# A selective scan over eight images a step in pairs: 128x1024 elementwise instructions, 16-step blocks and one shared double bank for rank-one terms

## The chip, the core and the metric

The kernel runs on one core of a Trainium2 chip. A core has engines that work side by side, each through its own list of instructions in order: TensorE (PE, with its weight loads PEld) for matmuls, VectorE (DVE), ScalarE (ACT) and GpSimd (POOL) for elementwise work, and SyncE (SP), which here issues most DMAs. They wait for one another through semaphores. Matmuls write PSUM[...]; the other tiles lie in SBUF. The metric is the device time of one execution in microseconds (us).

## What is computed

The input is eight images of 128 channels and 64 x 64 pixels. A layer with a deformable 3 x 3 convolution comes first: group norm, an offset convolution, bilinear gathers at the shifted positions, a convolution over nine taps, and a residual. Its result is read as 4096 tokens of 128 channels per image. Then a state-space scan runs over the tokens of each image, and last a mixture of eight experts, two of which are taken for each token.

```python
xs, z = jnp.split(x_proj, 2, axis=-1)            # x_proj = norm(t) @ W_in
delta = xs @ W_delta; Bv = xs @ W_B; Cv = xs @ W_C
deltaA = jnp.exp(jnp.einsum('bld,dn->bldn', delta, A))
deltaB = jnp.einsum('bld,bln->bldn', delta, Bv)
def step(state, inp):                             # state: images x 256 (d) x 256 (n)
    state = dA_i * state + dB_i * x_i[:, None, :]
    y = jnp.einsum('bdn,bn->bd', state, C_i)
y = y * silu(z);  t = t + y @ W_out
```

What takes the time is the scan: 4096 steps for every image, each of which multiplies a state of 256 x 256 values by decays, adds a term, and contracts the result with C.

## The kernel before

**Stages.** `prepare` and `images` run first. They build the gather table, offsets and weights of the deformable convolution for all images, and take the first 1.7 ms. Then the scan runs, for four images at a time (`QI = 4`), twice, each time over 128 blocks of 32 tokens (`BL = 32`). A block of 4 x 32 = 128 tokens fills the 128 partitions of the token work: `conv` gathers and convolves two blocks ahead, `project` computes xs, z, delta, B and C for the next block, and `behind` does the gate, the output projection, the router and the experts for the block before. A hardware loop covers `BODY = 32` blocks per pass, all written out.

**State and tiles.** The state index n lies on partitions, in two halves (`NH = 2`), and d (`DIN = 256`) along a row. So the state of one image is 128 x 512 fp32, one PSUM bank in size. The states of images 0, 1 and 2 are SBUF tiles `ht`; that of image 3 stays in PSUM, in `up[3]`.

**One step.**
- `decay` (L877, L883) computes dA. A matmul of `rt` (delta in three bf16 parts) with `alhs` (A in three bf16 parts) writes one of three rotating PSUM `bank`s, and ACT's Exp writes `et`. Nineteen such groups of 14 values of d serve one chunk, which is 16 (step, image) pairs; the groups are done one chunk ahead.
- `product` (L903) is `mt = et * h`, 128x512 per image. POOL does images 0 to 2, DVE image 3.
- `unit` (L897) computes the added term, B times delta times x, as a matmul with a contracted length of 9 (three by three bf16 parts) into the image's bank `up[b]`. The factors of image b lie on partitions 32b to 32b+8 of `ul` and `ur`. One call serves two images, in turn.
- `add` (L908) is `h = mt + up`, on DVE, 128x512 per image.
- `contract` (L916) adds C times `mt` into `yp`. Its stationary operand `zc` is a window of 32 columns that is zero except for one, which holds C; that column is chosen so that the result lands on the partition of this token. The part of the output that comes from the added term is put in later, through `qt` in `behind`.

**Order.** The order on each engine is written out by hand in `scan_block`: a step is cut into `NSLOT = 6` slots, each of which takes a decay group and one turn of the token work (`Work.step`, whose generators say with `yield n` how many slots later they go on). Between them stand the adds, contractions and rank-one terms. DMAs for the next chunk's factors (`load_u`, `load_r`) are issued on SP at a chunk's first step. `take` and `free` hand the three banks to token work and decays alike.

Of the kernel before, what the change touches and what calls it, by code (L numbers as in the profile page):

```python
# [23 lines left out]
FP = mybir.dt.float32  # L25
# [6 lines left out]
P = 128  # L32
# [7 lines left out]
DIN = 256  # L40
# [3 lines left out]
QI = 4  # L44
BL = 32
CH = 4
# [6 lines left out]
KR = 9 * GD  # L53
QP = 3
# [3 lines left out]
NSLOT = 6  # L58
# [6 lines left out]
def kernel(  # L65
# [76 lines left out]

    bp = [dram.tile([QI, 3, 3, BL, DIN], BF, name=f"bp{k}") for k in range(2)]
    dp = [dram.tile([QI, 3, 3, BL, DIN], BF, name=f"dp{k}") for k in range(2)]

# [266 lines left out]
    def several(n, shape, dt, name):  # L412
        return [fix.tile(shape, dt, name=f"{name}{k}") for k in range(n)]


    et = several(2, [P, NH, CH, QI, DIN], FP, "et")
    mt = several(3, [P, NH, QI, DIN], FP, "mt")
    ht = several(QP, [P, NH, DIN], FP, "ht")
    rt = several(2, [KR, RROW], BF, "rt")

    ul = several(2, [P, CH, DIN], BF, "ul")
    ur = several(2, [P, CH, DIN], BF, "ur")
    zc = several(2, [P, BL + 2, 32], FP, "zc")
# [6 lines left out]
    up = [psf.tile([P, NH, DIN], FP, name=f"up{k}") for k in range(QI)]  # L430
# [3 lines left out]
    for k in range(2):  # L434
        nc.vector.memset(ul[k], 0.0)
        nc.vector.memset(ur[k], 0.0)
        nc.gpsimd.memset(zc[k], 0.0)
# [16 lines left out]
    class Work:  # L454
# [3 lines left out]
        def add(self, gen, at=0):  # L458
            self.threads.append([gen, at])
# [139 lines left out]
    def project(k):  # L599
# [41 lines left out]
        for b in range(QI):  # L641
            for i in range(3):
                nc.sync.dma_start(
                    out=dp[k][b, i].rearrange("j l n -> l j n"),
                    in_=dpt[BL * b : BL * b + BL],
                )
# [48 lines left out]
        for b in range(QI):  # L695
            for j in range(3):
                nc.sync.dma_start(
                    out=bp[k][b, :, j].rearrange("i l n -> l i n"),
                    in_=bpt[BL * b : BL * b + BL],
                )  # L700
# [22 lines left out]
    def behind(b0, l0, k, kt):  # L723
# [40 lines left out]
        pr = wk[:, :NEXP]  # L764
        nc.vector.tensor_add(pr, pr, rb_sb)
        mx = one.tile([P, 1], FP, name="mx")
        nc.vector.tensor_reduce(mx, pr, AX.X, ALU.max)
        nc.vector.tensor_scalar(pr, pr, mx, None, ALU.subtract)
        yield 2
        nc.scalar.activation(pr, pr, AF.Exp)  # L770
        yield LAG
        sm = one.tile([P, 1], FP, name="sm")
        nc.vector.tensor_reduce(sm, pr, AX.X, ALU.add)
        nc.vector.reciprocal(sm, sm)
        nc.vector.tensor_scalar(pr, pr, sm, None, ALU.mult)
        yield 1
        top = one.tile([P, 2], FP, name="top")
        at = one.tile([P, 2], FP, name="at")
        hit = one.tile([P, NEXP], FP, name="hit")
        for kk in range(2):  # L780

            nc.vector.tensor_reduce(top[:, kk : kk + 1], pr, AX.X, ALU.max)
            nc.vector.scalar_tensor_tensor(
                hit, pr, top[:, kk : kk + 1], rank, ALU.is_equal, ALU.mult
            )
            nc.vector.tensor_reduce(at[:, kk : kk + 1], hit, AX.X, ALU.max)
            yield 1
            if kk == 0:

                nc.vector.tensor_scalar(hit, rank, at[:, 0:1], None, ALU.is_equal)  # L790
                nc.vector.scalar_tensor_tensor(pr, hit, -2.0, pr, ALU.mult, ALU.add)
                yield 1
        nc.vector.tensor_reduce(sm, top, AX.X, ALU.add)
        nc.vector.reciprocal(sm, sm)
        nc.vector.tensor_scalar(top, top, sm, None, ALU.mult)
        yield 1
        nc.vector.tensor_scalar(
            pr, rank, at[:, 0:1], top[:, 0:1], ALU.is_equal, ALU.mult
        )
        nc.vector.tensor_scalar(  # L800
            hit, rank, at[:, 1:2], top[:, 1:2], ALU.is_equal, ALU.mult
        )
        gate = one.tile([P, NEXP], FP, name="gate")
        nc.vector.tensor_add(gate, pr, hit)  # L804
# [48 lines left out]
    def load_u(k, c):  # L853
        rows = slice(CH * c, CH * c + CH)
        for b in range(QI):
            for dst, src in ((ul, bp), (ur, dp)):
                nc.sync.dma_start(
                    out=dst[c % 2][32 * b : 32 * b + 9],
                    in_=src[k][b, :, :, rows, :].rearrange("i j l n -> (i j) l n"),
                )  # L860

    def copy_c(k, c):

        nc.scalar.copy(
            zc[c % 2].rearrange("p s x -> p (s x)")[:, 31 : 31 + 32 * BL].rearrange(
                "p (s x) -> p s x", x=32
            )[:, :, 0].rearrange("p (m l) -> p m l", l=CH),
            ctt[k].rearrange("p h (b c l) -> p (h b) c l", b=QI, l=CH)[:, :, c, :],
        )

    def decay(c, g):

        n = min(GD, DIN - GD * g)
        ps = banks.pop(0)
        rv = rt[c % 2].rearrange("p (q g t) -> p q g t", q=GD, t=CT)[:, :n, g, :]
        for h in range(NH):
            nc.tensor.matmul(  # L877
                ps[:, n * CT * h : n * CT * h + n * CT].rearrange(
                    "p (q t) -> p q t", q=n
                ),  # L880
                alhs[:KR, g, P * h : P * h + P], rv, start=True, stop=True,
            )
        nc.scalar.activation(  # L883
            et[c % 2][:, :, :, :, GD * g : GD * g + n].rearrange(
                "p h l b d -> p h (l b) d"
            ),
            ps[:, : 2 * n * CT].rearrange("p (h d t) -> p h t d", h=NH, d=n),
            AF.Exp,
        )
        banks.append(ps)  # L890

    def unit(c, lo, images):

        for h in range(NH):
            for b in images:
                rows = slice(32 * b, 32 * b + 9)
                nc.tensor.matmul(  # L897
                    up[b][:, h], ul[c % 2][rows, lo, P * h : P * h + P],
                    ur[c % 2][rows, lo, :], start=True, stop=True,
                )  # L900

    def product(eng, m, c, lo, b):
        eng.tensor_tensor(  # L903
            mt[m][:, :, b], et[c % 2][:, :, lo, b], ht[b] if b < QP else up[b], ALU.mult
        )

    def add(m, b):
        nc.vector.tensor_tensor(  # L908
            ht[b] if b < QP else up[b], mt[m][:, :, b], up[b], ALU.add
        )  # L910

    def contract(m, lo, cpar, j):
        for h in range(NH):
            for b in range(QI):
                s0 = 32 * (CH * (QI * h + b) + lo) + 31 - j
                nc.tensor.matmul(  # L916
                    yp[32 * b : 32 * b + 32, :DIN],
                    zc[cpar].rearrange("p s x -> p (s x)")[:, s0 : s0 + 32],
                    mt[m][:, h, b, :],
                    start=(j == 0 and h == 0), stop=(j == BL - 1 and h == NH - 1),  # L920
                )

    def after(k, c, n):

        return ((k + (c + n) // NCH) % 2, (c + n) % NCH)
# [3 lines left out]
    def buf(j):  # L929

        n = BODY * BL
        return 1 if j == n - 1 and j % 3 == 0 else j % n % 3

    def scan_block(s, work):

        k = s % 2
        for c in range(NCH):
            for lo in range(CH):
                j = CH * c + lo
                m, m1 = buf(BL * s + j), buf(BL * s + j + 1)  # L940
                cn, ln = (c, lo + 1) if lo + 1 < CH else (c + 1, 0)
                if lo == 0:
                    load_u(*after(k, c, 1))
                    load_r(*after(k, c, 2))
                for b in range(QP):
                    product(nc.gpsimd, m, c, lo, b)

                def slot(s):
                    g = NSLOT * lo + s
                    if g < NG:  # L950
                        decay((c + 1) % NCH, g)
                    work(NSLOT * j + s)

                add(m, 0)
                slot(0)
                add(m, 1)
                if last:
                    contract(*last.pop())
                slot(1)
                unit(c % 2, lo, (2, 3))  # L960
                slot(2)
                if lo == 0:
                    copy_c(*after(k, c, 1))
                add(m, 2)
                slot(3)
                unit(cn % 2, ln, (0, 1))
                add(m, 3)
                slot(4)
                product(nc.vector, m1, cn, ln, 3)
                slot(5)  # L970
                last.append((m, lo, c % 2, j))
# [5 lines left out]
    for b0 in range(0, NB, QI):  # L977
# [4 lines left out]
        for b in range(QP):  # L982
            nc.vector.memset(ht[b], 0.0)
        nc.vector.memset(up[3], 0.0)
# [6 lines left out]
        product(nc.vector, 0, 0, 0, 3)  # L991
        unit(0, 0, (0, 1))
# [57 lines left out]
```

## Time and profile before

| | |
|---|---|
| median of 3 runs | 40915.19 us (40786.07 to 40924.38) |
| profiled execution | 40839.57 us, its span 40837.8 us |
| busy share of the span | PE 88%, POOL 81%, DVE 73%, ACT 60% |
| mean granted TensorE clock | 0.914 |
| first and last add of the scan (L908) | 1727 us and 40803 us into the span |
| DMA | 3935 MB, mean busy share of the 16 engines about 0.33 |

In the profile a line such as `L916 PE MATMUL yp<-mt,zc ... x131072 | 9629.5, 415` names the source line, engine, operation, output and inputs, and the number of instructions; behind the bar stand the time in which at least one of them was running (us) and the mean duration of one (ns), then the engine's idle time just before them and what ended it. Matmuls are pipelined: their durations overlap, and how long one keeps PE from the next is seen from the distance of starts in the timeline.

### The profile page before, as it was taken

How to read it: one execution, taken by the hardware profiler on the slowest of the kernel's cores; microseconds unless marked ns; L12 is line 12 of the kernel's file. 1: busy time of each engine (PE TensorE's matmuls, PEld its weight loads, DVE VectorE, ACT ScalarE, POOL GpSimd, SP SyncE). 2: the span in 40 equal slices, each digit the busy share in tenths (PEclk: the TensorE clock that was granted, in tenths of full speed). 3: DMA queues.
4: the chain of work that ended last, by engine and by line, in shares of the span. 5: the costliest groups of instructions: out<-in, count | busy, mean ns of one | idle time of the engine just before them, and what ended most of it. 6: DMA issues, size and time to landing. Idle time of an engine off the chain costs nothing. (4 is left out here: it accounts for less than half of the span.)

```text
span 40837.8 us, 930352 instructions
## 1 busy us (share of the span) xinstructions
PE 35932.1 (88%) x339020; PEld 18203.8 (45%) x339020; DVE 29992.8 (73%) x57416; ACT 24575.6 (60%) x61837; POOL 33028.2 (81%) x26997
## 2 busy tenths in 40 slices
PE   3599998999988999899989999889998999989898
PEld 1244444444444444444444444444444444444444
DVE  1377777777777777777777777777777777777777
ACT  0266666666666666666666666666666666666666
POOL 0388888888888888888878888888888888888888
PEclk7799999999999999999989999999999999999999
DMA  3333333333333333333333333333333333333333
GB/s 87 82 98 96 96 98 95 99 97 97 97 97 100 96 96 98 97 96 100 97 97 97 96 97 99 95 99 98 97 97 97 96 95 97 97 94 98 100 99 92
DMA packets 3069459, 3935.38 MB, mean 96 GB/s; under 512 B 1764375, under 2 KB 2499040, under 8 KB 2804848
## 3 DMA queue, kind: packets, MB, share of 16 engines
q1 hardware_dynamic: 2797344, 3200.76, 26.9%
q0 software_dynamic: 187200, 613.57, 5.2%
q10 hardware_dynamic: 80328, 61.56, 0.6%
q8 instruction: 2675, 43.83, 0.5%
q14 instruction: 1912, 15.66, 0.1%
HBM read 3276.01 MB, written 598.31 MB: 95 GB/s over the span
## 5 line engine op out<-in xcount | busy, mean ns | idle before, releaser
L903 POOL TENSOR_TENSOR mt<-et,ht 128x512 f32<-128x512 f32 x24576 | 30657.2, 1275 | 5715.9 <-DVE ht L908 4556.4
L883 ACT ACTIVATE et<-bank 128x448 f32<-128x448 f32 (+1 forms) x38950 | 19947.9, 537 | 10341.7 <-PE bank L877 9450.6
L908 DVE TENSOR_TENSOR ht<-mt,up 128x512 f32<-128x512 f32 x24576 | 16236.0, 682 | 8427.5 <-PE up L897 7118.0
L877 PE MATMUL bank<-rt,alhs 126*128 126x224 bf16 (+1 forms) x77900 | 13427.6, 266 | 2371.5 <-ACT et L883 1147.7
L877 PEld LDWEIGHTS <-alhs 126*128 126x128 bf16 x77900 | 6094.4, 99 | 10397.5 <-issue 9937.4
L916 PE MATMUL yp<-mt,zc 128*32 128x256 f32 x131072 | 9629.5, 415 | 0.0
L897 PE MATMUL up<-ur,ul 9*128 9x256 bf16 x65544 | 6919.2, 284 | 763.1 <-DVE ht L908 429.3
L903 DVE TENSOR_TENSOR mt<-et,up 128x512 f32<-128x512 f32 x8194 | 5618.5, 686 | 430.7 <-ACT et L883 26.6
L908 DVE TENSOR_TENSOR up<-mt,up 128x512 f32<-128x512 f32 x8192 | 5638.4, 688 | 4.2 <-PE bank L877 4.2
L916 PEld LDWEIGHTS yp<-mt,zc 128*32 128x32 f32 x131072 | 3687.0, 115 | 3130.1 <-issue 1326.3
L897 PEld LDWEIGHTS <-ul 9*128 9x128 bf16 x65544 | 1973.8, 93 | 4834.8 <-issue 4459.1
L574 PE MATMUL bank<-ident,w 128*128 128x128 f32 x18720 | 3390.5, 307 | 442.4 <-ACT et L883 312.7
L566 ACT ACTIVATE w<-g,rec 128x128 f32<-128x128 f32 x9360 | 3622.5, 397 | 125.7 <-DMA g<-table,rec 120.4
L574 PEld LDWEIGHTS bank<-ident,w 128*128 128x128 f32 x18720 | 2620.1, 202 | 1210.2 <-ACT et L883 565.8
L545 POOL DMA_INDIRECT g<-table,rec x2340 | 2312.3, 988 | 463.5 <-issue 207.5
L658 PE MATMUL bank<-xst,wdelta_sb 128*32 128x128 f32 x20640 | 1821.2, 426 | 67.1 <-ACT et L883 67.1
L580 ACT COPY vt<-bank 128x128 f32<-128x128 f32 x2340 | 618.8, 264 | 1914.2 <-PE bank L574 1868.2
L818 ACT ACTIVATE se<-bank,gate 128x128 f32<-128x128 f32 x2048 | 714.9, 364 | 446.3 <-PE bank L812 372.6
L289 POOL MEMSET xpad<- 128x66 f32 x8 | 1.2, 153 | 1210.8 <-POOLq L256 1210.8
L812 PE MATMUL bank<-ew_sb,tn2t 128*128 128x256 f32 x2048 | 918.7, 544 | 32.3 <-DVE gate L804 21.7
L277 PE MATMUL gm_ps<-mv,gavg 128*128 128x1 f32 x16 | 4.5, 347 | 906.9 <-DVE mv L275 906.9
L522 PE MATMUL bank<-wconv_sb,vt 128*128 128x128 f32 x4680 | 708.4, 287 | 0.0
(200 smaller groups left out, 16661.2 us busy)
## 6 DMA issues: line engine op xcount, KB each, us to landing
rt<-rz SPq DMA_DIRECT2D x2052, 1102.5 KB
rz<-dst SPq DMA_DIRECT2D x3096, 52.5 KB
dp<-dpt SPq DMA_DIRECT2D x3096, 48.0 KB
bp<-bpt SPq DMA_DIRECT2D x3096, 48.0 KB
ul<-bp SPq DMA_DIRECT2D x8200, 18.0 KB
ur<-dp SPq DMA_DIRECT2D x8200, 18.0 KB
g<-table,rec POOLq DMA_INDIRECT x2340
table<-xtok SPq DMA_DIRECT2D x256, 128.0 KB
```

Of the source, the lines that this page charges most:

```text
L545: nc.gpsimd.indirect_dma_start(out=g, out_offset=None, in_=table, in_offset=bass.IndirectOffsetOnAxis(ap=rec.bitcast(I32)[:, j : j + 1], a ...
L566: nc.scalar.activation(w[:, P * q : P * q + P], g[:, P * q : P * q + P], AF.Copy, scale=rec[:, c0 : c0 + 1],)
L574: nc.tensor.matmul(wk[:, :P], w[:, P * q : P * q + P], ident, start=(q == 0), stop=(q == 3),)
L658: nc.tensor.matmul(wk[32 * a : 32 * a + 32, P * gg : P * gg + P], wdelta_sb[:, h, d0 : d0 + 32], xlb[:, h], start=(h == 0), stop=(h == 1),)
L812: nc.tensor.matmul(wk[:, :DIN], tn2t, ew_sb[:, DIN * hf : DIN * hf + DIN], start=True, stop=True,)
L818: nc.scalar.activation(se[:, ex, :], wk[:, P * j : P * j + P], AF.Copy, scale=gate[:, ex : ex + 1],)
L877: nc.tensor.matmul(ps[:, n * CT * h : n * CT * h + n * CT].rearrange("p (q t) -> p q t", q=n), alhs[:KR, g, P * h : P * h + P], rv, start= ...
L883: nc.scalar.activation(et[c % 2][:, :, :, :, GD * g : GD * g + n].rearrange("p h l b d -> p h (l b) d"), ps[:, : 2 * n * CT].rearrange("p ...
L897: nc.tensor.matmul(up[b][:, h], ul[c % 2][rows, lo, P * h : P * h + P], ur[c % 2][rows, lo, :], start=True, stop=True,)
L903: eng.tensor_tensor(mt[m][:, :, b], et[c % 2][:, :, lo, b], ht[b] if b < QP else up[b], ALU.mult)
L908: nc.vector.tensor_tensor(ht[b] if b < QP else up[b], mt[m][:, :, b], up[b], ALU.add)
L916: nc.tensor.matmul(yp[32 * b : 32 * b + 32, :DIN], zc[cpar].rearrange("p s x -> p (s x)")[:, s0 : s0 + 32], mt[m][:, h, b, :], start=(j == ...
```

## The change

All eight images now go through the scan at once, in four pairs, and blocks are 16 steps long, so that a block is still 128 tokens. There are 4096 steps of eight images in place of 8192 steps of four. `product` and `add` handle two images in one 128x1024 instruction. POOL does pairs 0 to 2; pair 3 keeps its state in two PSUM banks `ud`. The rank-one terms of pairs 0, 1 and 2 all go through the same two banks, `up`, one pair after another, where each image had a bank before. The factors of both images of a pair lie on the same nine partitions, 32p to 32p+8, of one tile `uu`. `contract` is called for each pair, and writes rows 32p to 32p+31 of `yp`: 16 rows for each image. `mt` becomes four tiles of a pair each, and `md` for pair 3. A chunk is two steps of eight images, so a decay group still covers 16 (step, image) pairs; a step has 12 slots. In the router, small tiles move into PSUM, and two masks are kept instead of two ranks. The start of the scan, with a block of token work on its own, runs once instead of twice.

```diff
-QI = 4
-BL = 32
-CH = 4
+QI = 8
+BL = 16
+CH = 2
...
-NSLOT = 6
+NSLOT = 12
...
-    et = several(2, [P, NH, CH, QI, DIN], FP, "et")
-    mt = several(3, [P, NH, QI, DIN], FP, "mt")
-    ht = several(QP, [P, NH, DIN], FP, "ht")
+    et = several(2, [P, CH, QI, NH, DIN], FP, "et")
+    mt = several(4, [P, 2, NH, DIN], FP, "mt")
+    md = fix.tile([P, 2, NH, DIN], FP, name="md")
+    ht = several(QP, [P, 2, NH, DIN], FP, "ht")
...
-    up = [psf.tile([P, NH, DIN], FP, name=f"up{k}") for k in range(QI)]
+    ud = psf.tile([P, 2, NH, DIN], FP, name="ud")
+    up = psf.tile([P, 2, NH, DIN], FP, name="up")
...
     def load_u(k, c):
-        rows = slice(CH * c, CH * c + CH)
-        for b in range(QI):
-            for dst, src in ((ul, bp), (ur, dp)):
-                nc.sync.dma_start(
-                    out=dst[c % 2][32 * b : 32 * b + 9],
-                    in_=src[k][b, :, :, rows, :].rearrange("i j l n -> (i j) l n"),
-                )
+        for p in range(NP):
+            nc.sync.dma_start(
+                out=uu[c % 2][32 * p : 32 * p + 9].rearrange("r w b l n -> r (w b) (l n)"),
+                in_=pr[k].rearrange("i j p w b l n -> p (i j) (w b) (l n)")[
+                    p, :, :, CH * DIN * c : CH * DIN * c + CH * DIN
+                ],
+            )
...
-    def unit(c, lo, images):
+    def unit(c, lo, p):
+        rows = slice(32 * p, 32 * p + 9)
         for h in range(NH):
-            for b in images:
-                rows = slice(32 * b, 32 * b + 9)
+            for b in range(2):
                 nc.tensor.matmul(
-                    up[b][:, h], ul[c % 2][rows, lo, P * h : P * h + P],
-                    ur[c % 2][rows, lo, :], start=True, stop=True,
-                )
+                    (up if p < QP else ud)[:, b, h],
+                    uu[c % 2][rows, 0, b, lo, P * h : P * h + P],
+                    uu[c % 2][rows, 1, b, lo, :], start=True, stop=True,
+                )
...
-    def contract(m, lo, cpar, j):
+    def contract(j, c, lo, p):
+        r = j % BL
         for h in range(NH):
-            for b in range(QI):
-                s0 = 32 * (CH * (QI * h + b) + lo) + 31 - j
+            for b in range(2):
+                s0 = 32 * (CH * (QI * h + 2 * p + b) + lo) + 31 - (BL * b + r)
                 nc.tensor.matmul(
-                    yp[32 * b : 32 * b + 32, :DIN],
-                    zc[cpar].rearrange("p s x -> p (s x)")[:, s0 : s0 + 32],
-                    mt[m][:, h, b, :],
-                    start=(j == 0 and h == 0), stop=(j == BL - 1 and h == NH - 1),
+                    yp[32 * p : 32 * p + 32, :DIN],
+                    zc[c % 2].rearrange("p s x -> p (s x)")[:, s0 : s0 + 32],
+                    buf(j, p)[:, b, h, :],
+                    start=(r == 0 and h == 0 and b == 0),
+                    stop=(r == BL - 1 and h == NH - 1 and b == 1),
                 )
...
+                    if sl == 0:
+                        product(j, c, lo, 3)
+                        if last:
+                            contract(*last.pop())
+                    elif sl == 1:
+                        unit(c, lo, 0)
+                    elif sl == 3:
+                        unit(c, lo, 3)
+                        add(j, 0)
+                    elif sl == 4:
+                        contract(j, c, lo, 0)
+                    elif sl == 5:
+                        add(j, 3)
+                        unit(c, lo, 1)
+                    elif sl == 6:
+                        contract(j, c, lo, 3)
+                    elif sl == 7:
+                        add(j, 1)
+                        if lo == 0:
+                            copy_c(*after(k, c, 1))
+                    elif sl == 8:
+                        contract(j, c, lo, 1)
+                    elif sl == 9:
+                        unit(c, lo, 2)
+                    elif sl == 11:
+                        add(j, 2)
+                        last.append((j, c, lo, 2))
```

In the router (`behind`) the instructions of L795 and L800, which read and write small SBUF tiles, are replaced by ones with an operand in PSUM:

```diff
-        nc.vector.tensor_scalar(
-            hit, rank, at[:, 1:2], top[:, 1:2], ALU.is_equal, ALU.mult
-        )
+        nc.vector.tensor_scalar(hit, mask[:, 0, :], top[:, 0:1], None, ALU.mult)
```

More of the change, by code (lines that the diff above doesn't have):

```diff
@@ L53 @@
 KR = 9 * GD
+NP = QI // 2
 QP = 3
@@ L141 @@
     adr = dram.tile([DIN, 3, DIN], BF, name="adr")
-    bp = [dram.tile([QI, 3, 3, BL, DIN], BF, name=f"bp{k}") for k in range(2)]
-    dp = [dram.tile([QI, 3, 3, BL, DIN], BF, name=f"dp{k}") for k in range(2)]
+    pr = [dram.tile([3, 3, NP, 2, 2, BL, DIN], BF, name=f"pr{k}") for k in range(2)]
     rz = [
@@ L413, in several @@
         return [fix.tile(shape, dt, name=f"{name}{k}") for k in range(n)]
-    et = several(2, [P, NH, CH, QI, DIN], FP, "et")
-    mt = several(3, [P, NH, QI, DIN], FP, "mt")
-    ht = several(QP, [P, NH, DIN], FP, "ht")
+    et = several(2, [P, CH, QI, NH, DIN], FP, "et")
+    mt = several(4, [P, 2, NH, DIN], FP, "mt")
+    md = fix.tile([P, 2, NH, DIN], FP, name="md")
+    ht = several(QP, [P, 2, NH, DIN], FP, "ht")
     rt = several(2, [KR, RROW], BF, "rt")
-    ul = several(2, [P, CH, DIN], BF, "ul")
-    ur = several(2, [P, CH, DIN], BF, "ur")
-    zc = several(2, [P, BL + 2, 32], FP, "zc")
+    uu = several(2, [P, 2, 2, CH, DIN], BF, "uu")
+    zc = several(2, [P, NH * QI * CH + 2, 32], FP, "zc")
     ctt = several(2, [P, NH, P], FP, "ctt")
@@ L434 @@
     for k in range(2):
-        nc.vector.memset(ul[k], 0.0)
-        nc.vector.memset(ur[k], 0.0)
+        nc.vector.memset(uu[k], 0.0)
         nc.gpsimd.memset(zc[k], 0.0)
@@ L640, in project @@
         free()
-        for b in range(QI):
+        for p in range(NP):
             for i in range(3):
                 nc.sync.dma_start(
-                    out=dp[k][b, i].rearrange("j l n -> l j n"),
-                    in_=dpt[BL * b : BL * b + BL],
+                    out=pr[k].rearrange("i j p w b l n -> i p w (b l) j n")[i, p, 1],
+                    in_=dpt[32 * p : 32 * p + 32],
                 )
@@ L694, in project @@
         free()
-        for b in range(QI):
+        for p in range(NP):
             for j in range(3):
                 nc.sync.dma_start(
-                    out=bp[k][b, :, j].rearrange("i l n -> l i n"),
-                    in_=bpt[BL * b : BL * b + BL],
+                    out=pr[k].rearrange("i j p w b l n -> j p w (b l) i n")[j, p, 0],
+                    in_=bpt[32 * p : 32 * p + 32],
                 )
@@ L763, in behind @@
         yield LAG
[L764 to L768, printed above, removed]
+        pr_, hit = wk[:, :NEXP], wk[:, NEXP : 2 * NEXP]
+        top, at = wk[:, 16:18], wk[:, 18:20]
+        sm, mx = wk[:, 20:21], wk[:, 21:22]
+        mask = one.tile([P, 2, NEXP], FP, name="mask")
+        nc.vector.tensor_add(pr_, pr_, rb_sb)
@@ L769, in behind @@
+        nc.vector.tensor_reduce(mx, pr_, AX.X, ALU.max)
+        nc.vector.tensor_scalar(pr_, pr_, mx, None, ALU.subtract)
         yield 2
-        nc.scalar.activation(pr, pr, AF.Exp)
+        nc.scalar.activation(pr_, pr_, AF.Exp)
         yield LAG
-        sm = one.tile([P, 1], FP, name="sm")
-        nc.vector.tensor_reduce(sm, pr, AX.X, ALU.add)
+        nc.vector.tensor_reduce(sm, pr_, AX.X, ALU.add)
         nc.vector.reciprocal(sm, sm)
-        nc.vector.tensor_scalar(pr, pr, sm, None, ALU.mult)
@@ L776, in behind @@
         yield 1
-        top = one.tile([P, 2], FP, name="top")
-        at = one.tile([P, 2], FP, name="at")
-        hit = one.tile([P, NEXP], FP, name="hit")
+        nc.vector.tensor_scalar(pr_, pr_, sm, None, ALU.mult)
+        yield 1
         for kk in range(2):
-            nc.vector.tensor_reduce(top[:, kk : kk + 1], pr, AX.X, ALU.max)
+            nc.vector.tensor_reduce(top[:, kk : kk + 1], pr_, AX.X, ALU.max)
             nc.vector.scalar_tensor_tensor(
-                hit, pr, top[:, kk : kk + 1], rank, ALU.is_equal, ALU.mult
+                hit, pr_, top[:, kk : kk + 1], rank, ALU.is_equal, ALU.mult
@@ L785, in behind @@
             )
+            yield 1
             nc.vector.tensor_reduce(at[:, kk : kk + 1], hit, AX.X, ALU.max)
+            nc.vector.tensor_scalar(
+                mask[:, kk, :], hit, at[:, kk : kk + 1], None, ALU.is_equal
+            )
             yield 1
             if kk == 0:
-                nc.vector.tensor_scalar(hit, rank, at[:, 0:1], None, ALU.is_equal)
-                nc.vector.scalar_tensor_tensor(pr, hit, -2.0, pr, ALU.mult, ALU.add)
-                yield 1
+                nc.vector.scalar_tensor_tensor(
+                    pr_, mask[:, 0, :], -2.0, pr_, ALU.mult, ALU.add
+                )
@@ L793, in behind @@
         nc.vector.tensor_reduce(sm, top, AX.X, ALU.add)
         nc.vector.reciprocal(sm, sm)
+        yield 1
         nc.vector.tensor_scalar(top, top, sm, None, ALU.mult)
+        nc.vector.tensor_scalar(hit, mask[:, 0, :], top[:, 0:1], None, ALU.mult)
         yield 1
-        nc.vector.tensor_scalar(
-            pr, rank, at[:, 0:1], top[:, 0:1], ALU.is_equal, ALU.mult
-        )
-        nc.vector.tensor_scalar(
-            hit, rank, at[:, 1:2], top[:, 1:2], ALU.is_equal, ALU.mult
-        )
@@ L803, in behind @@
-        gate = one.tile([P, NEXP], FP, name="gate")
-        nc.vector.tensor_add(gate, pr, hit)
+        gate = one.tile([P, NEXP], FP, name="gate")
+        nc.vector.scalar_tensor_tensor(
+            gate, mask[:, 1, :], top[:, 1:2], hit, ALU.mult, ALU.add
+        )
         free()
@@ L853, in load_u @@
     def load_u(k, c):
-        rows = slice(CH * c, CH * c + CH)
-        for b in range(QI):
-            for dst, src in ((ul, bp), (ur, dp)):
-                nc.sync.dma_start(
-                    out=dst[c % 2][32 * b : 32 * b + 9],
-                    in_=src[k][b, :, :, rows, :].rearrange("i j l n -> (i j) l n"),
-                )
+        for p in range(NP):
+            nc.sync.dma_start(
[3 more added lines that the diff above has]
+                ],
+            )
     def copy_c(k, c):
         nc.scalar.copy(
-            zc[c % 2].rearrange("p s x -> p (s x)")[:, 31 : 31 + 32 * BL].rearrange(
+            zc[c % 2].rearrange("p s x -> p (s x)")[:, 31 : 31 + 32 * NH * QI * CH].rearrange(
                 "p (s x) -> p s x", x=32
@@ L884, in decay @@
             et[c % 2][:, :, :, :, GD * g : GD * g + n].rearrange(
-                "p h l b d -> p h (l b) d"
+                "p l b h d -> p h (l b) d"
             ),
@@ L890, in decay, with buf, product, add @@
         banks.append(ps)
-    def unit(c, lo, images):
+    def unit(c, lo, p):
+        rows = slice(32 * p, 32 * p + 9)
         for h in range(NH):
-            for b in images:
-                rows = slice(32 * b, 32 * b + 9)
+            for b in range(2):
                 nc.tensor.matmul(
-                    up[b][:, h], ul[c % 2][rows, lo, P * h : P * h + P],
-                    ur[c % 2][rows, lo, :], start=True, stop=True,
-                )
-    def product(eng, m, c, lo, b):
-        eng.tensor_tensor(
-            mt[m][:, :, b], et[c % 2][:, :, lo, b], ht[b] if b < QP else up[b], ALU.mult
-        )
-    def add(m, b):
-        nc.vector.tensor_tensor(
-            ht[b] if b < QP else up[b], mt[m][:, :, b], up[b], ALU.add
-        )
-    def contract(m, lo, cpar, j):
+                    (up if p < QP else ud)[:, b, h],
+                    uu[c % 2][rows, 0, b, lo, P * h : P * h + P],
+                    uu[c % 2][rows, 1, b, lo, :], start=True, stop=True,
+                )
+    def buf(j, p):
+        return mt[(QP * j + p) % 4] if p < QP else md
+    def product(j, c, lo, p):
+        (nc.gpsimd if p < QP else nc.vector).tensor_tensor(
+            buf(j, p), et[c % 2][:, lo, 2 * p : 2 * p + 2],
+            ht[p] if p < QP else ud, ALU.mult,
+        )
+    def add(j, p):
+        if p < QP:
+            nc.vector.tensor_tensor(ht[p], buf(j, p), up, ALU.add)
+        else:
+            nc.vector.tensor_tensor(ud, md, ud, ALU.add)
+    def contract(j, c, lo, p):
+        r = j % BL
         for h in range(NH):
-            for b in range(QI):
-                s0 = 32 * (CH * (QI * h + b) + lo) + 31 - j
+            for b in range(2):
+                s0 = 32 * (CH * (QI * h + 2 * p + b) + lo) + 31 - (BL * b + r)
                 nc.tensor.matmul(
-                    yp[32 * b : 32 * b + 32, :DIN],
-                    zc[cpar].rearrange("p s x -> p (s x)")[:, s0 : s0 + 32],
-                    mt[m][:, h, b, :],
-                    start=(j == 0 and h == 0), stop=(j == BL - 1 and h == NH - 1),
+                    yp[32 * p : 32 * p + 32, :DIN],
[3 more added lines that the diff above has]
+                    stop=(r == BL - 1 and h == NH - 1 and b == 1),
                 )
@@ L927 @@
     last = []
-    def buf(j):
-        n = BODY * BL
-        return 1 if j == n - 1 and j % 3 == 0 else j % n % 3
     def scan_block(s, work):
@@ L938, in scan_block @@
             for lo in range(CH):
-                j = CH * c + lo
-                m, m1 = buf(BL * s + j), buf(BL * s + j + 1)
-                cn, ln = (c, lo + 1) if lo + 1 < CH else (c + 1, 0)
+                j0 = CH * c + lo
+                j = BL * s + j0
                 if lo == 0:
@@ L944, in scan_block @@
                     load_r(*after(k, c, 2))
[L945 to L949, printed above, removed]
+                for p in range(QP):
+                    product(j, c, lo, p)
+                for sl in range(NSLOT):
+                    g = NSLOT * lo + sl
                     if g < NG:
                         decay((c + 1) % NCH, g)
[L952 to L971, printed above, removed]
+                    work(NSLOT * j0 + sl)
+                    if sl == 0:
[25 more added lines that the diff above has]
+                        last.append((j, c, lo, 2))
     def run(gen):
@@ L981 @@
         run(conv(b0, BL, 1))
-        for b in range(QP):
-            nc.vector.memset(ht[b], 0.0)
-        nc.vector.memset(up[3], 0.0)
+        for p in range(QP):
+            nc.vector.memset(ht[p], 0.0)
+        nc.vector.memset(ud, 0.0)
         load_r(0, 0)
@@ L990 @@
             decay(0, g)
-        product(nc.vector, 0, 0, 0, 3)
-        unit(0, 0, (0, 1))
         with tc.For_i(0, NBLOCK * BL, BODY * BL) as i0:
```

## The prediction

> **What bounds the kernel now.** I read the page first, for the shares and the groups of the scan.
>
> ```profile
> span 40837.8 us, 930352 instructions
> ...
> PE 35932.1 (88%) x339020; PEld 18203.8 (45%) x339020; DVE 29992.8 (73%) x57416; ACT 24575.6 (60%) x61837; POOL 33028.2 (81%) x26997
> ...
> L903 POOL TENSOR_TENSOR mt<-et,ht 128x512 f32<-128x512 f32 x24576 | 30657.2, 1275 | 5715.9 <-DVE ht L908 4556.4
> ...
> L908 DVE TENSOR_TENSOR ht<-mt,up 128x512 f32<-128x512 f32 x24576 | 16236.0, 682 | 8427.5 <-PE up L897 7118.0
> ...
> L916 PE MATMUL yp<-mt,zc 128*32 128x256 f32 x131072 | 9629.5, 415 | 0.0
> L897 PE MATMUL up<-ur,ul 9*128 9x256 bf16 x65544 | 6919.2, 284 | 763.1 <-DVE ht L908 429.3
> ```
>
> PE and POOL are both nearly full, and they are coupled through DVE: POOL's products wait for DVE's adds, the adds wait for PE's rank-one terms. The L916 row is the odd one: 131072 x 415 ns is 54 ms, but the group was busy 9.6 ms, so its matmuls overlap, more than five deep. Each fp32 matmul call is two passes in the trace (131072 passes for 65536 calls).
>
> Next, the step time: busy time and counts by stretch, for DVE's one product a step (L903; the counts are in brackets).
>
> ```profile
> core 0: us, DVE busy (x) POOL busy (x), PEclk, DMA share, GB/s
> 21300.00:40800.00 19500.00, 2808.55 (x4096) 15326.96 (x12287) 0.92 0.33 97
> ```
>
> 19500 / 4096 = 4.76 us a step of four images, so 9.52 us for eight image-steps, which is the new unit of work. Of that POOL works 6 x 1.275 + 0.56 of gathers (2312 us / 4096) = 8.2 us.
>
> Busy time of a pipelined PE says little, so I took starts from the timeline of PE over one step (start, duration, line, count).
>
> ```profile
> 20005.81 1.07 PE L916 MATMUL yp<-mt,zc 128*32 128x256 f32 x16
> 20006.82 0.37 PE L877 MATMUL bank<-rt,alhs 126*128 126x224 bf16 x2
> 20007.02 0.61 PE L522 MATMUL bank<-wdelta_sb,xst 128*128 128x256 f32 x2
> 20007.56 0.39 PE L897 MATMUL up<-ur,ul 9*128 9x256 bf16 x4
> 20007.89 0.56 PE L877 MATMUL bank<-rt,alhs 126*128 126x224 bf16 x4
> ```
>
> Start to next start: sixteen contraction passes 1.01 us, a decay pair 0.20, four rank-one passes 0.33. Asked for narrow windows (20000.00 to 20000.05, then 20000.30 to 20000.35), the same timeline lists only the passes running then:
>
> ```profile
> 20000.03 0.42 PE L916 MATMUL yp<-mt,zc 128*32 128x256 f32 x4
> ...
> 20000.03 0.64 PE L916 MATMUL yp<-mt,zc 128*32 128x256 f32 x8
> ```
>
> One round of four ends after 0.42 us, two after 0.64: each further round of four adds 0.22.
>
> Last, what one column group costs when nothing runs beside it: the front stage has nine calls (18 passes) of 512 columns into the same 27 output partitions.
>
> ```profile
> 331.84 7.91 PE L333 MATMUL op<-xpad,woff_sb 128*27 128x512 f32 x18
> 339.68 0.42 PE L344 MATMUL omp<-ident,om_t 27*128 27x27 f32 x4
> ```
>
> 7.84 / 18 = 0.436 us for 512 columns, 0.218 for 256: as long as a whole round of four in the scan. A narrow pass is no cheaper; the scan's contraction is cheap because four go side by side.
>
> [...] 1.01 - 4 x 0.22 = 0.13 us after a contraction, 0.33 - 2 x 0.115 = 0.10 after a rank-one group, and 0.09 before either (four decay passes take 0.49 before L897 where two pairs are 0.40). [...] the scan is granted 0.92, the front stage at 333 to 341 us, 27 columns wide and dense, 1.00.
>
> **The change part by part**, for eight image-steps.
>
> *Contraction.* Before, one call of contract writes images 0 to 3 into yp strips 0, 32, 64, 96: per half of the state four column groups at once. Two calls cost 2 x (1.01 + 0.09) = 2.2 us. After, a call serves one pair, and its four calls all write yp[32p:32p+32]: one strip, eight passes in a row, 8 x 0.218 = 1.74, plus drains 0.13 + 0.09 = 1.97. Four pairs: 7.9 us. Pairs are separated in PE's order by decay and rank-one matmuls, so strips of two pairs don't meet. Added: 5.7 us.
>
> *Rank-one terms.* Before, images 2 and 3 (then 0 and 1) sit on different 32-row strips and overlap: four groups of 0.33 + 0.09 = 1.7 us. After, both images of a pair use rows 32p: four passes in a row. A 256-column bf16 pass is 0.20 / 2 x 256 / 224 = 0.115; 4 x 0.115 + 0.10 + 0.09 = 0.65, four pairs 2.6 us. Added: 0.9 us.
>
> *Unchanged on PE.* Decay: 9.5 pairs x 0.20 = 1.9. The 256 token blocks' own matmuls: about 18720 + 12400 + 2100 + 3000 passes of 128 columns and a quarter of L658's 20640, at 0.128 (eight in 1.03 us at 330.81), and 6200 of 256 at 0.22, some 6.7 ms, 1.65 us a unit.
>
> PE's own sum: before 1.9 + 2.2 + 1.7 + 1.65 = 7.45 of 9.52 us, 2.1 us lost to waits and slow clock. After: 1.9 + 7.9 + 2.6 + 1.65 = 14.05 us.
>
> *Products and adds in 128x1024.* POOL: no such row. At most 2 x 1.275 = 2.55; [...] 3 x 2.35 + 0.56 = 7.6 us. DVE: at most 2 x 0.69; [...] Five of them and about 0.55 of block work make 6.6 us. ACT: 9.5 x 0.55 + 1.1 = 6.3. All are gains (0.6 us on POOL, 0.75 on DVE) under a PE of 14 us, so worth nothing; without that cover they would be worth about 0.6.
>
> *Router rewrite.* It drops the long L800 and L795 (1224 and 824 ns, 0.52 ms in all) on DVE: hidden likewise, worth 0.5 ms at most.
>
> *DMA.* Loads of rank-one factors fall from eight to four per chunk at equal bytes, rec loads rise from four to eight a block, runs of xt and out halve to 64 B. DMA share is 0.33, and a chunk will last 29 us, not 19: hidden. SP has fewer instructions queued ahead of rt. At a share of 1 it would count; it is far off.
>
> *One shared `up`.* unit(p) must wait until add(p-1) has read it. Behind that wait stands everything on PE. Between each add's release and the next unit PE has a contraction or two (1.97 each) or, at the turn of the step, slots 10, 11, 0 with one: over 2.5 us, against 1.22 plus the semaphores. Hidden; if not, up to 1.5 us three times.
>
> *Outer loop.* One prologue instead of two: the gap at 21220 is 106 us, those between bodies 26, so 80 us less. Seven body gaps stay.
>
> *Waits of PE left over.* Bounds: 0 and the 2.1 us of before. Most of those belonged to adds and products that are now early; ACT's evictions remain where slots without contraction follow each other. I take 0.5.
>
> Sum: 4096 x 14.55 = 59.6 ms, front 1.73 ms (first scan add at 1727 us), gaps and tail about 0.2: 61.5 ms. The working stands against 40839.6 us of the profiled execution, 0.2% under the median of 40915; I shift nothing.
>
> **Rivals.** *Passes of one strip overlap after all* (0.05): the four calls of a pair pipeline deeper than a strip of the front stage does. At the old price per image PE needs 14.05 - 5.7 = 8.4 us, and with coupling as before (9.52 against POOL's 8.2) a unit is about 8.9: 38.3 ms, faster. It decides below some 0.85 us per pair instead of 1.97. For it: overlapping sums in the L916 row; against: 0.436 per pass at L333, and rounds of 0.22.
>
> *Turns on the shared double bank are bare* (0.08): every unit waits for its add, 14.05 + 3 x 1.5 = 18.5 us, 77.8 ms. For it: the adds' largest wait is already for PE; against: the contractions that stand between.
>
> *The throttle* (0.04) [...] 28 us a unit, 117 ms. Against: the 27-column stage at 1.00.
>
> **Numbers.** The forecast, PE bound by serial strips, has 0.82: 61,500 us. Its range: no waits and prices 4% lower, 13.6 us, 57,600; waits of 2.0, 16.05 us, 67,700. That holds nearly all of its 0.82, so it is the range too. Within 0.5% counts as no change, about what this measurement can tell; no case lands there, I leave 0.01. Faster 0.04, slower 0.95.
>
> **What would show it.** The PE row nearly full with no idle left; a contraction group of eight passes spanning about 1.75 us, L916's successor with busy near 4096 x 32 x 0.22 = 29 ms; rank-one groups near 0.5; POOL about half busy at 2.35 per product, waiting for DVE adds; DVE adds waiting for PE; granted clock above 0.95. I am wrong if contraction passes start 7 ns apart, if PE idles on `up`, or if PEclk falls towards 0.5.

## The result, and the profile after

The changed kernel takes 58325.49 us (median of four runs, 58321.75 to 58327.11) against 40862.28 us before (median of four runs here): 1.4275 times as long, with a 95% interval of 1.4244 to 1.4305. The forecast was 61,500 us in a range of 57,600 to 67,700: the time lies inside, 0.7 ms above its lower end.

The page of the changed kernel has these lines in place of those shown of before.

```profile
span 58319.9 us, 865360 instructions
...
PE 56507.0 (97%) x338676; PEld 28790.7 (49%) x338676; DVE 28282.2 (48%) x36888; ACT 25466.6 (44%) x61704; POOL 31168.3 (53%) x14691
...
L911 POOL TENSOR_TENSOR mt<-et,ht 128x1024 f32<-128x1024 f32 x12288 | 28841.4, 2357 | 25032.8 <-DVE ht L918 13863.5
...
L918 DVE TENSOR_TENSOR ht<-mt,up 128x1024 f32<-128x1024 f32 x12288 | 15001.5, 1221 | 25544.5 <-PE up L900 25340.5
L927 PE MATMUL yp<-mt,zc 128*32 128x256 f32 x98304 | 23526.3, 382 | 0.0
...
L927 PE MATMUL yp<-md,zc 128*32 128x256 f32 x32768 | 7842.9, 382 | 0.0
L900 PE MATMUL up<-uu 9*128 9x256 bf16 x49152 | 7445.4, 270 | 0.0
```

POOL and DVE did become cheaper: POOL was busy 30.7 ms with 24576 products of 1275 ns, and is busy 28.8 ms with 12288 of 2357 ns; the adds on `ht` went from 16.2 to 15.0 ms. It is of no use: POOL now idles 25 ms before its products, 13.9 of them until DVE's adds, and these wait 25 ms for PE. The contraction has as many passes as before (98304 + 32768 = 131072), yet its busy time went from 9.6 to 31.4 ms. The zeros at the end of the L900 and L927 rows say that PE did not stand idle before them: neither the shared double bank nor a product held it up.

The stretch of the scan, counted as before by DVE's one product a step:

```profile
2000.00:57000.00 55000.00, 4831.22 (x3981) 28033.58 (x11945) 1.00 0.22 67
```

55000 / 3981 = 13.82 us for eight image-steps, where it was 9.52, at full TensorE clock (the 1.00; 0.92 before). The timeline of PE over part of a step shows where it is:

```profile
30043.10 0.36 PE L880 MATMUL bank<-rt,alhs 126*128 126x224 bf16 x2
30043.39 1.91 PE L927 MATMUL yp<-mt,zc 128*32 128x256 f32 x8
30045.24 0.37 PE L880 MATMUL bank<-rt,alhs 126*128 126x224 bf16 x2
30045.54 0.61 PE L900 MATMUL up<-uu 9*128 9x256 bf16 x4
30046.08 0.36 PE L880 MATMUL bank<-rt,alhs 126*128 126x224 bf16 x2
30046.37 1.91 PE L927 MATMUL yp<-md,zc 128*32 128x256 f32 x8
30048.22 0.56 PE L880 MATMUL bank<-rt,alhs 126*128 126x224 bf16 x4
```

Eight passes into one strip hold PE for 1.85 us (30043.39 to 30045.24); before, sixteen passes over four strips held it for 1.01. The start before it gives the time lost ahead of a group, which the prediction counts among its drains: the decay pair at 30043.10 is followed after 0.29 us, where 0.20 is its own. What PE does in this 0.09 us no trace shows; "drain" stands below for such a time, here and behind a group, and for nothing more.

### The profile page after: what moved, and what is told of

Read it like the earlier page. It is cut to its first block, busy times and chain, and to the rows that moved or that the text cites. A ratio compares the mean times of both kernels' runs of the same rounds, so it can differ in the third digit from the quotient of the medians.

```text
span 58319.9 us, 865360 instructions
## 1 busy us (share of the span) xinstructions
PE 56507.0 (97%) x338676; PEld 28790.7 (49%) x338676; DVE 28282.2 (48%) x36888; ACT 25466.6 (44%) x61704; POOL 31168.3 (53%) x14691
## 5 line engine op out<-in xcount | busy, mean ns | idle before, releaser
L911 POOL TENSOR_TENSOR mt<-et,ht 128x1024 f32<-128x1024 f32 x12288 | 28841.4, 2357 | 25032.8 <-DVE ht L918 13863.5
L918 DVE TENSOR_TENSOR ht<-mt,up 128x1024 f32<-128x1024 f32 x12288 | 15001.5, 1221 | 25544.5 <-PE up L900 25340.5
L927 PE MATMUL yp<-mt,zc 128*32 128x256 f32 x98304 | 23526.3, 382 | 0.0
L927 PEld LDWEIGHTS yp<-mt,zc 128*32 128x32 f32 x98304 | 9863.5, 110 | 9610.8 <-issue 1724.7
L927 PE MATMUL yp<-md,zc 128*32 128x256 f32 x32768 | 7842.9, 382 | 0.0
L900 PE MATMUL up<-uu 9*128 9x256 bf16 x49152 | 7445.4, 270 | 0.0
L900 PEld LDWEIGHTS <-uu 9*128 9x128 bf16 x65536 | 4822.9, 92 | 4105.8 <-issue 3096.9
L920 DVE TENSOR_TENSOR ud<-md,ud 128x1024 f32<-128x1024 f32 x4096 | 5015.5, 1224 | 1089.1 <-PE ud L900 1084.5
L911 DVE TENSOR_TENSOR md<-et,ud 128x1024 f32<-128x1024 f32 x4096 | 4970.8, 1214 | 94.7 <-PEq L1004 83.6
L927 PEld LDWEIGHTS yp<-md,zc 128*32 128x32 f32 x32768 | 3295.6, 110 | 3070.0 <-issue 326.1
L900 PE MATMUL ud<-uu 9*128 9x256 bf16 x16384 | 2482.9, 270 | 0.0
```

The lines of the kernel that those rows point to most:

```text
L900: nc.tensor.matmul((up if p < QP else ud)[:, b, h], uu[c % 2][rows, 0, b, lo, P * h : P * h + P], uu[c % 2][rows, 1, b, lo, :], start=True ...
L911: (nc.gpsimd if p < QP else nc.vector).tensor_tensor(buf(j, p), et[c % 2][:, lo, 2 * p : 2 * p + 2], ht[p] if p < QP else ud, ALU.mult,)
L918: nc.vector.tensor_tensor(ht[p], buf(j, p), up, ALU.add)
L920: nc.vector.tensor_tensor(ud, md, ud, ALU.add)
L927: nc.tensor.matmul(yp[32 * p : 32 * p + 32, :DIN], zc[c % 2].rearrange("p s x -> p (s x)")[:, s0 : s0 + 32], buf(j, p)[:, b, h, :], start= ...
```

## The experiments

The theory is that of serial strips, and rests on two times of the kernel before: 0.218 us for a pass of 256 columns where all go into the same 27 output partitions (L333), and 0.22 for a round of four passes into four strips (L916). It says that passes into the same 32 partitions of the output, or from the same 32 rows, take their turns, and that those of different strips run side by side. Its rivals are that the cost comes with the number of groups and drains, and that the turns on the shared double bank make PE wait. Steps are measured as above.

**Four strips for one pair's contraction.** Only the strip that a call writes to is changed, with the flags for the first and last matmul of a sum.

```diff
-                    yp[32 * p : 32 * p + 32, :DIN],
+                    yp[32 * (2 * h + b) : 32 * (2 * h + b) + 32, :DIN],
```

> The changed kernel with one thing different: the four contraction calls of a pair write to the four different 32-partition strips of yp instead of all to strip 32p. The number, size, order and buffers of all instructions stay. It adds up C's results in other rows of yp than the reference, so its output is another computation and only its time is read. Theory of serial strips: eight passes of a pair take two rounds of 0.216 us instead of eight, so 1.3 us less for each of four pairs, 5.2 us of the measured 13.8 us a step; PE then needs about 8.6 us, POOL 7.6, and a step takes 8.6 to 9.3 us: 37,300 to 40,200 us. Rival, the cost lies in having four separate groups with a drain around each instead of one: nothing changes, 58,300 us. Rival, the turns on the shared double bank: PE waits where it now works, and the time stays above 50,000 us.

Measured: 44494.33 us, 10.44 us a step. At 30020 us, where the decay pair ahead of it takes 0.29 us as in the changed kernel at a clock of 1.00, a group does what was expected:

```profile
30019.98 0.36 PE L880 MATMUL bank<-rt,alhs 126*128 126x224 bf16 x2
30020.27 0.64 PE L927 MATMUL yp<-mt,zc 128*32 128x256 f32 x8
30020.84 0.37 PE L880 MATMUL bank<-rt,alhs 126*128 126x224 bf16 x2
```

Its eight passes hold PE for 0.57 us in place of 1.85, 5.1 us for four pairs. Both rivals fall: with the same groups and passes 3.4 us of a step are gone. But that is less than 5.1, and the time lies above the range. The granted clock fell to 0.84; more on that below.

**Two strips of rows for a pair's rank-one terms.** Image i's factors move to row strip i mod 4, so that the two images of a pair lie on different ones; the layout of `pr` in DRAM follows.

```diff
-        rows = slice(32 * p, 32 * p + 9)
...
+                q, s = divmod(2 * p + b, NP)
+                rows = slice(32 * s, 32 * s + 9)
```

> The changed kernel, with the factors of the two images of a pair on different 32-row strips of the array (image i on strip i mod 4), so that the four rank-one passes of a pair can overlap two by two as they did before. Contraction untouched. Theory of serial strips (rows as well as columns): a group goes from 0.65 to 0.42 us, four groups 0.92 us less of 13.8 us a step: 54,550 us, between 54,000 and 55,200. Rival, rank-one passes never cost by strips but by their number: no change, 58,300 us.

Measured: 55354.07 us, just above the range. The group itself did what was expected. In the timeline of this run:

```profile
30036.21 0.39 PE L901 MATMUL up<-uu 9*128 9x256 bf16 x4
30036.53 0.36 PE L880 MATMUL bank<-rt,alhs 126*128 126x224 bf16 x2
```

It holds PE for 0.32 us, 0.54 in the changed kernel, so four save 0.88 a step; of these 0.73 arrived ((58325 - 55354) / 4096). So the forecast's rank-one term is shown too, and in these two runs rows count for about a sixth of what columns do (0.88 against 5.1 us of PE work a step).

**All four pairs contracted together**, at the start of the next step, in turn over the pairs; the calls at slots 4, 6 and 8 go.

```diff
+        for h, b, p in [(h, b, p) for h in range(NH) for b in range(2) for p in range(NP)]:
```

> The changed kernel, with the contractions of all four pairs of a step issued together at the start of the next step, in turn over the pairs, so that the four strips of yp run side by side; same buffers, same number of matmuls, result as in the reference. Theory of serial strips: 32 passes in eight rounds of 0.216 plus one drain pair, 1.95 us instead of 7.66 a step, so PE needs 8.1 us; POOL needs 7.6 and may wait for the buffers that are held for longer: 8.1 to 9.5 us a step, 35,200 to 41,000 us. Rival, the shared double bank: with less work between a unit and the add before it, PE now waits on the bank three times a step, and the step stays near 10 to 12 us, 43,000 to 51,000 us.

Measured: 63969.97 us, outside both ranges, at a granted clock of 0.70. The edit left the products of the next step ahead of the contraction in the program, and with four buffers these overwrite pairs 0 and 1 first. So contraction waited for the next step's products and took those in (its output is another computation on that account, and only its time is read). Its waits:

```profile
DVE md L911 <- PE yp L926: 24938.3, 4080, 9.3
...
PE yp L926 <- POOL mt L911: 8314.2, 5947, 3.2
```

It tells nothing of strips, but shows a wait at the head of PE's work, 8.3 ms in all: behind it in the program stood decays and rank-one terms, and behind those DVE. How much of the time is due to the wait and how much to the clock was not separated. The same with rank-one terms on two strips, whose contraction has the same fault:

> Both edits together: all four pairs contracted side by side, and rank-one factors of a pair on two row strips. Theory of serial strips: PE needs 7.2 us a step and is no longer the longest; POOL's 7.6 with the coupling sets the step, 7.8 to 9.2 us: 34,000 to 39,700 us, below the kernel before. Rival, the shared double bank binds once contractions no longer cover it: no faster than the version with contractions alone, and not below 40,900 us.

Measured: 60435.82 us, at a clock of 0.76: outside its range too.

**The same with the products in their place**: those of pairs 1 and 2 are issued behind the contraction that reads the buffers they take.

```diff
-                for p in range(QP):
-                    product(j, c, lo, p)
+                product(j, c, lo, 0)
...
                             contract(*last.pop())
-                        product(j, c, lo, 3)
+                        for p in (3, 1, 2):
+                            product(j, c, lo, p)
```

> As the version with all contractions together, but with the products of pairs 1 and 2 issued behind the contraction of the step before, so that this reads the products of its own step as in the reference. Theory of serial strips with the throttle: PE needs 8.1 us a step at full clock; the version with the four calls in four strips needed about 8.65 and took 10.4 at a granted clock of 0.84, so with a clock of 0.85 to 0.95 this takes 8.6 to 9.8 us: 37,200 to 42,200 us. Rival, what held that version was the shared double bank and not the clock: here even less work stands between an add and the next unit, so 10.5 to 12 us a step, 45,000 to 51,000 us.

Measured: 47286.05 us. And with rank-one terms on two strips:

> The version before with rank-one factors on two row strips as well. Serial strips with the throttle: PE needs 7.2 us at full clock, POOL 7.6; 8.0 to 9.3 us a step, 34,800 to 40,100 us. Rival, shared double bank: no gain over the version before, 45,000 us or more.

Measured: 43888.38 us. Both are much faster than the changed kernel, and both slower than I expected. The rival's time came in the first, but the shared bank is not the longest wait there: PE waits 2.5 ms for it, POOL 13.0 ms for the contraction. The waits of the second, longest first:

```profile
ACT et L886 <- PE bank L880: 14087.8, 12431, 5.1
DVE md L912 <- PE yp L927: 10515.2, 4069, 5.2
POOL mt L912 <- PE yp L927: 10188.5, 3340, 6.6
...
PE up L901 <- DVE ht L919: 3401.8, 3048, 3.5
```

ACT's wait for decays was there before (23.9 ms in the changed kernel). The next two are new: DVE and POOL wait 10.5 and 10.2 ms for the contraction to give their buffers free, because products are now held until all four pairs are there. The shared bank is a third of either (3.4 ms). The clock is part of it as well: it was 0.83 in the first and 0.87 in the second, where PE also stood idle for 10% and 14% of the scan (2000 to 37000 us). What each of these costs was not separated, and no run had more buffers.

**Pairs p and p+4.** Without any new buffer, a pair that joins distant images has two column strips and two row strips, since rows 16i of `yp` belong to image i.

```diff
-            buf(j, p), et[c % 2][:, lo, 2 * p : 2 * p + 2],
+            buf(j, p), et[c % 2][:, lo, p::NP],
...
+                s, q = divmod(p + NP * b, 2)
...
-                    yp[32 * p : 32 * p + 32, :DIN],
+                    yp[32 * s : 32 * s + 32, :DIN],
```

> The changed kernel with images p and p+4 as pair p in place of 2p and 2p+1. Strips, buffers, slots and numbers of instructions stay, but the two images of a pair then lie on two column strips of yp and two row strips of the factors. Serial strips: eight passes in four rounds instead of eight, 0.86 us less for each of four pairs, and rank-one groups 0.23 less each: 13.8 - 4.4 = 9.4 us of PE work a step; at a clock of 0.92 to 1.00 9.4 to 10.2 us: 40,500 to 43,800 us. Rival, number of groups and drains: no change, 58,300 us.

Measured: 42491.55 us, 1.0433 times before (1.0406 to 1.046), at a clock of 0.98: inside the range. Four groups with a drain each are still there; only their strips are doubled.

```profile
30022.74 1.06 PE L929 MATMUL yp<-mt,zc 128*32 128x256 f32 x8
30023.73 0.36 PE L880 MATMUL bank<-rt,alhs 126*128 126x224 bf16 x2
```

Eight passes hold PE for 0.99 us here, 1.85 on one strip and 0.57 on four: four, eight and two rounds of 0.216 us, and each time about 0.13 us more.

**Two groups of two pairs**, so that all four strips are used and no product waits for more than one other.

```diff
                     elif sl == 6:
-                        contract(j, c, lo, 3)
+                        contract(j, c, lo, (0, 3))
...
-                        last.append((j, c, lo, 2))
+                        last.append((j, c, lo, (1, 2)))
```

> The version with pairs p and p+4, with pairs 0 and 3 contracted together at slot 6 and pairs 1 and 2 together at the start of the next step, so that each of two groups a step uses all four column strips; the product of pair 2 is issued behind the second group, whose buffer it takes. Serial strips: two groups of four rounds, 2 x 1.07 = 2.1 us instead of 4 x 1.07 = 4.3, so PE work falls from 9.4 to 7.3 us a step and POOL's 7.6 is the longest. With the waits and the clock seen so far 8.2 to 9.5 us: 35,600 to 40,900 us. Rival, with PE's contraction off, waits between engines and a lower granted clock take the gain, as in the version with all pairs together: 9.5 to 10.4 us, 40,900 to 44,600 us, with a clock under 0.9.

Measured: 39560.73 us, 0.9709 times before (0.9686 to 0.9732): inside the range, and below the rival's, at a clock of 0.94.

**The first group directly behind the rank-one terms of pair 1.**

```diff
                     elif sl == 5:
                         add(j, 3)
                         unit(c, lo, 1)
-                    elif sl == 6:
                         contract(j, c, lo, (0, 3))
```

> The same, with the first contraction group directly behind the rank-one terms of pair 1, without a decay and token work between them. [...] on the other side decay work that hid ACT's evictions moves. Serial strips with drains: 0 to 0.2 us a step faster than the version before, 0 to 800 us. Rival, waits decide and not PE work: within 200 us of it, or slower.

Measured: 38921.58 us, 0.9555 times before (0.9533 to 0.9577), and 640 us under the one before it: inside the 0 to 800 that were expected, outside the rival's 200. PE's busy time fell by 0.5 ms; what one drain less brings alone was not measured. With two contraction groups for eight image-steps, as many as the kernel before has, the change as a whole was worth 2.9%. The 1.6% of this last step come from an order in which the kernel before was not tried. Its page:

```profile
PE 34420.2 (88%) x338676; PEld 17651.5 (45%) x338676; DVE 27929.2 (72%) x36888; ACT 24507.6 (63%) x61704; POOL 31146.9 (80%) x14691
```

Here PE and POOL have the shares that they had in the kernel before, with POOL's work 1.9 ms less.

**The order within a group, in the kernel before.** Images outside, halves inside: two calls in a row share a strip.

```diff
-        for h in range(NH):
-            for b in range(QI):
+        for b in range(QI):
+            for h in range(NH):
```

> The kernel before with one thing different: contract goes through its eight calls with images outside and halves inside, so that two calls in a row share a strip. Theory of serial strips, with PE taking matmuls in their order: four passes a strip stand in a row, 13 gaps of 0.216 us in place of 3, 1.9 to 2.1 us more PE work a step of four images; 3.7 + 2.0 = 5.7 us, with waits 5.7 to 6.3 us where it is 4.76: 48,400 to 53,500 us. Rival, [...] only the set of strips counts: no change, 40,900 us.

Measured: 40761.58 us, 1.0001 times before (0.9989 to 1.0012). I was wrong, and the rival's time came. The timeline:

```profile
20010.35 1.09 PE L916 MATMUL yp<-mt,zc 128*32 128x256 f32 x16
20011.37 0.41 PE L897 MATMUL up<-ur,ul 9*128 9x256 bf16 x8
```

Sixteen passes hold PE for 1.02 us, where it was 1.01. With the same four strips in the group, the order of its calls made no difference here; how PE gets there, the trace doesn't tell.

**Clock or waits in the run with four strips.** The same edit with two strips for each pair, `yp[64 * (p % 2) + 32 * h : ...]`.

> The changed kernel, with the four contraction calls of a pair written to two strips of yp, two calls each, where the earlier run had four strips; like that one it adds up in other rows than the reference, and only its time is read. Eight passes then take four rounds, 0.43 us more for each pair than with four strips: PE work 8.7 + 1.7 = 10.4 us a step at full clock. Theory of serial strips with the throttle (what the run with four strips lacked was clock, granted 0.84, and denser work brings it back to 0.97 or more): 10.4 to 10.8 us a step, 44,600 to 46,300 us, within 4% of the run with four strips. Rival, that run was held by waits between engines, to which PE's passes come on top: 10.4 + 1.7 = 12.1 us a step, 51,500 us, clock about 0.85.

Measured: 45645.03 us, 10.72 us a step, at a clock of 0.99. Twice the rounds, 7 ms more work of PE at full clock (an estimate, 4096 x 4 x 0.43 us), cost 1.2 ms. This lies inside the range, and far from the rival's 51,500. So the gain that the four-strip run lacked had gone with its clock (0.84 against 0.99), and not to waits on top of which PE's work comes.

## Why the prediction was right

Its deciding step, the contraction, is shown by the first run, in which nothing but the strips of `yp` was changed and 14 ms went. The pairs p and p+4, with which images form a pair and the row strips changed as well, took 16 ms off. That passes into one strip take their turns was right (eight held PE for 1.85, 0.99 and 0.57 us on one, two and four strips); the total was 5% too high, as PE's sum and the waits were both put too large. Term by term:

- *Contraction.* 1.74 + 0.13 for eight passes and the drain after them; measured 1.85. A drain of 0.09 ahead of them; measured 0.09.
- *Rank-one terms.* 0.46 + 0.10; measured 0.54, and taken back by the run with two row strips.
- *PE's sum and waits.* 14.05 + 0.5 us a step; measured 13.82 in all, of which 0.18 is PE's idle time in the scan. So the waits were 0.3 too high and PE's sum 0.4. A good half of the latter is contraction that ran side by side where two pairs met without a decay between, in the last slots of every second step: about 4600 of 115,000 neighbouring pass starts are closer than 0.1 us, which saves 1 ms in all, 0.24 us a step. I had said that strips of two pairs don't meet.
- *Wide instructions.* 2.35 us on POOL and 1.22 us on DVE were my estimates, which no trace of before shows (it has 1275 and 682 ns at 512 columns); measured 2.357 and 1.221. They were hidden, as the waits show. What they are worth without that cover I put at 0.6 us a step; the last of the tuned versions has 9.08 (35500 us for 3910 steps) against 9.52, 0.44 less with all parts of the change together and the contraction in its new place.
- *The shared double bank.* Costed at nothing, and PE was not idle before L900 in the changed kernel. With the cover gone it does cost something: PE waits 1.3 ms on it in the fastest version, 3.4 ms in the one with all pairs together.
- *The rivals.* Passes of one strip did not overlap: 0.216 us from start to start. With serial strips the granted clock did not fall towards a half: it was 0.99, where the kernel before had 0.914. It was lower in several versions with less work on PE (0.84 with four strips for a pair), which I had not foreseen.
- *DMA and router.* DMA share fell to 0.22. The router was not tried on its own.

## What to carry to other kernels

When pairs or larger units are formed to make elementwise instructions wider, look at where their parts lie on the matmul array: in this kernel narrow outputs and short contractions were cheap only where the passes of a group lay on different strips (eight contraction passes 0.57 us on four strips, 1.85 on one; four rank-one passes 0.32 on two, 0.54 on one). The busy time of a group divided into the sum of its durations gives a first hint of how many ran at once (5.6 before, 1.6 with one strip, where passes of 382 ns start 216 ns apart and so still overlap), and a place in the same profile where a narrow matmul runs alone gives the price of losing that (L333 before, 0.436 us for a pass of 512 columns). Choose the members of a pair so that they fall on different strips (here p and p+4), and group contractions no further than the buffers allow.

## What the runs showed of the hardware

Two things I had not expected. The order of matmul calls within a group did not matter: with two calls in a row to the same strip, four strips still ran side by side (1.02 us for sixteen passes, 1.0001 times the time).

And the granted clock was a half in stretches of a run in which PE was busy nearly all the time. The run with four strips, with PE busy for 94% of its span and a mean granted clock of 0.84, has stretches like these (columns: length, DVE products, POOL products, clock, DMA):

```profile
7310.70:7379.00 68.30, 6.06 (x5) 36.62 (x16) 0.50 0.30 83
17694.00:17813.00 119.00, 15.76 (x13) 90.14 (x40) 1.00 0.36 104
```

A step takes about 13.7 us in the first, at a clock of 0.50, and 9.2 in the second, at 1.00. Over the runs the clock did not follow the busy share of PE alone: it was 0.84 here at 94%, 0.94 in the fastest version at 88%, 0.914 in the kernel before at 88%, and 0.99 in the changed kernel at 97%. With two strips for each pair in place of four, which the expectation calls denser work, it was 0.99. What the granted clock goes by is not settled by these runs.
